# Convolution taps cut to the image, and half of fc1's second half as fifteen quarter-block products with banks that go on as sums

## The chip, the cores and the metric

The kernel runs on one core of one Trainium2 chip. The metric is the device time of one execution in microseconds; before the change its median over three runs is 3315.44 us (3314.96 to 3315.86). All data are float32.

## The reference, cut to what matters

Two layers over 8 images of 384 channels and 32 x 32 pixels (1024 tokens).

```python
# layer 0, per image: attention, then an MLP
xn   = layernorm(x, g1, beta1)
x1   = x + proj(attention(xn))                 # 8 heads of 48
xn2  = layernorm(x1, g2, beta2)
h    = gelu(einsum('bnc,oc->bno', xn2, w_fc1) + b_fc1)     # fc1: 384 -> 1536
x    = x1 + einsum('bnh,oh->bno', h, w_fc2) + b_fc2        # fc2: 1536 -> 384

# layer 1, per image: ConvNeXt block with global response norm
y = conv(x, dw_w, 7x7, padding 3, one filter per channel) + dw_b
y = layernorm over channels(y)
y = gelu(y @ w1 + b1)                          # 384 -> 1536
y = gamma * (y * nx) + beta + y                # nx: norms of the columns over their mean
x = x + (y @ w2 + b2)                          # 1536 -> 384
```

## The kernel before

Tokens lie along the free dimension, channels on the 128 partitions: an image is three channel tiles of 128 x 1024, and `NH` is 512, half of the tokens. The hidden layer is `HT` = 12 tiles of 128 rows. Instructions are issued in program order on each engine. Work of other engines is woven between TensorE's products by a clock in the program (`flow`), which counts the expected TensorE time: `flow.pe(us)` moves it on, and a generator yields the time until its next step. `U` = 0.857 us is one 128 x 128 by 128 x 512 matmul.

The convolution adds one tap at a time on VectorE from a copy of the image with a border of zeros (`pad`). Of the 49 taps, the last seven (`HELPED`) of each channel tile are done by ScalarE (multiply) and GpSimd (a DMA that adds); `taken` keeps VectorE from the channel tile that they are at.

```python
def convolution(acc, us, first=(), y0=0, y1=H, ready=tuple(range(CT)), taken=None):
    done = [0] * CT
    ct, n = None, 0
    taps = KS * KS - (HELPED if taken is not None else 0)
    while min(done) < taps:
        left = [c for c in ready if done[c] < taps and not (taken and taken.get(c, 0) > flow.now)]
        ...
        i = done[ct]
        dy, dx = divmod(i, KS)
        window = pad[:, ct, dy + y0 : dy + y1, dx : dx + W]
        dst = image(acc[:, ct, :])[:, y0:y1, :]
        tap = col("dww", ct * KS * KS + i)
        ...
            nc.vector.scalar_tensor_tensor(dst, window, tap, dst, ALU.mult, ALU.add)
        ...
        yield next((early for m, early in first if n <= m), us)
```

The MLP makes the hidden tiles for the first half of the tokens, then for the second; each half tile is three matmuls into one bank of `ps_o` (four banks), and a gelu on ScalarE. `difference` makes two operands for fc2 ahead of it.

```python
def gelu_half(hid, m, h, xn, weights, wname, name):
    w = weights.at(wname, m // CM)[:, m % CM * CT : (m % CM + 1) * CT, :]
    ps = linear_half(lambda k: w[:, k, :], lambda k: xn[:, k, :], CT, h, f"{name}_{h}_{m}")
    other_table(hid[:, m, half(h)], ps, AF.Gelu, bias=bfc1[:, m : m + 1])

def difference(dst, more, less):
    nc.scalar.mul(dst, less, -1.0)
    nc.gpsimd.dma_start(out=dst, in_=more, accum_op=ALU.add)

def mlp(b, xt, xn, weights, tag, ln, rest, before_fc2=None, behind_ln=None):
    ...
    for m in range(HT):
        gelu_half(hid, m, 0, xn, weights, wa, f"fc1_{b}")
        if m == 3 and rest:
            rest()                  # the projection of the second half, then its norm, ln
            ...
            behind_ln(ln)           # the norm behind the convolution waits for ln
    flow.finish(ln)
    for m in range(HT):
        gelu_half(hid, m, 1, xn, weights, wa, f"fc1_{b}")
        if m % CM == CM - 1:
            weights.used(wa, m // CM)
        if m in (3, 5):
            two_tiles = hid[:, m - 3 : m - 1, :]
            difference(e[(m - 3) // 2], two_tiles[:, :, half(0)], two_tiles[:, :, half(1)])
    ...                             # fc2, by thirds: 15 products of four matmuls for 18
```

The fc2 and w2 products already use sums of weight blocks (15 products for 18); image 0 makes these forms once (`forms`) and stores them. Weights come through a ring of nine buffers (`weights`). The last image (7) has an MLP of its own by halves, and a convolution in two parts of rows (0 to 13, 13 to 32) whose pace is 0.66 and 0.86 us a tap.

Of the kernel before, what the change touches and what calls it, by code (L numbers as in the profile page):

```python
# [46 lines left out]
F32 = mybir.dt.float32  # L47
AF = mybir.ActivationFunctionType
ALU = mybir.AluOpType
# [15 lines left out]
CM = 2  # L65
NC = HT // CM
U = 0.857
HELPED = 7
SCALE = HD ** -0.5
EPS0, EPS1, GRN_EPS = 1e-5, 1e-6, 1e-6  # L70
# [81 lines left out]
def block_kernel(  # L152
# [25 lines left out]
    flow = Flow()  # L178
    quiet = []
    s_fc2 = dram.tile([P, len(FORMS), 4 * P], F32, tag="s_fc2", bufs=1, name="s_fc2")  # L180
    s_w2 = dram.tile([P, len(FORMS), 4 * P], F32, tag="s_w2", bufs=1, name="s_w2")
    s_qk = dram.tile([P, CT, 4 * P], F32, tag="s_qk", bufs=1, name="s_qk")
    s_w1 = dram.tile([P, HT // 2, 4, P], F32, tag="s_w1", bufs=1, name="s_w1")

    def half(h):
        return slice(h * NH, (h + 1) * NH)
# [103 lines left out]
    def chunk(w, c):  # L290
        return w[:, c * 6 * P : (c + 1) * 6 * P]
# [3 lines left out]

    def plan_fc1(tag):
        return [((f"fc1_{tag}", c), chunk(wfc1, c)) for c in range(NC)]

    def plan_fc2(tag):
        return [((f"fc2_{tag}", a), chunk(wfc2, c)) for c, a in enumerate(RAW)]  # L300
# [491 lines left out]
    def add_first(xt, r, n, bank):  # L792
        dst = xt[:, r, half(n)]
        nc.vector.scalar_tensor_tensor(dst, bank, col("bfc2", r), dst, ALU.add, ALU.add)  # L794

    def mlp(b, xt, xn, weights, tag, ln, rest, before_fc2=None, behind_ln=None):

        hid = one.tile([P, HT * N], F32, tag="big", name=f"hid_{b}").rearrange("p (m n) -> p m n", m=HT)
        e = [three.tile([P, 2, NH], F32, tag="p", name=f"fc2_e_{b}_{i}") for i in range(2)]
        wa = f"fc1_{tag}"  # L800
        flow.finish(ln)
        for m in range(HT):
            gelu_half(hid, m, 0, xn, weights, wa, f"fc1_{b}")
            if m == 3 and rest:
                rest()
                slow = 1.2 if b == 1 else 1.0
                ln = flow.spawn(layernorm(xt, xn, 1, eps0, "g2", f"ln2_{b}", True, slow=slow))
                behind_ln(ln)
        flow.finish(ln)
        for m in range(HT):  # L810
            gelu_half(hid, m, 1, xn, weights, wa, f"fc1_{b}")
            if m % CM == CM - 1:
                weights.used(wa, m // CM)
            if m in (3, 5):
                two_tiles = hid[:, m - 3 : m - 1, :]
                difference(e[(m - 3) // 2], two_tiles[:, :, half(0)], two_tiles[:, :, half(1)])
        if before_fc2:
            before_fc2()
        bias = lambda r: col("bfc2", r)
        by_thirds(xt, hid, e, True, weights, f"fc2_{tag}", bias, lambda r, n: pad_half(xt, r, n), f"fc2_{b}")  # L820
# [132 lines left out]
    def keep(b, xt):  # L953
# [2 lines left out]
        nc.sync.dma_start(out=kept.rearrange("(c p) n -> p c n", p=P), in_=xt)  # L956
        return kept

    def convolution(acc, us, first=(), y0=0, y1=H, ready=tuple(range(CT)), taken=None):

        done = [0] * CT
        ct, n = None, 0
        taps = KS * KS - (HELPED if taken is not None else 0)
        while min(done) < taps:
            left = [c for c in ready if done[c] < taps and not (taken and taken.get(c, 0) > flow.now)]
            if not left:
                yield 1.0
                continue  # L970
            ct = min([c for c in left if c != ct] or left, key=lambda c: done[c])
            i = done[ct]
            dy, dx = divmod(i, KS)
            window = pad[:, ct, dy + y0 : dy + y1, dx : dx + W]
            dst = image(acc[:, ct, :])[:, y0:y1, :]
            tap = col("dww", ct * KS * KS + i)
            if i == 0:
                nc.vector.tensor_scalar(dst, window, tap, col("dwb", ct), ALU.mult, ALU.add)  # L978
            else:
                nc.vector.scalar_tensor_tensor(dst, window, tap, dst, ALU.mult, ALU.add)  # L980
            done[ct] += 1
            n += 1
            yield next((early for m, early in first if n <= m), us)

    def help_convolution(acc, us, taken):

        yield 8.0
        for ct in reversed(range(CT)):
            taken[ct] = float("inf")
            for i in range(KS * KS - HELPED, KS * KS):  # L990
                dy, dx = divmod(i, KS)
                for h in range(2):
                    if quiet:
                        while quiet:
                            yield 1.0
                        yield 3.0
                    t = three.tile([P, NH], F32, tag="res", bufs=4, name=f"tap_{ct}_{i}_{h}")
                    y0 = dy + h * H // 2
                    window = pad[:, ct, y0 : y0 + H // 2, dx : dx + W]
                    tap = col("dww", ct * KS * KS + i)  # L1000
                    nc.scalar.mul(t.rearrange("p (h w) -> p h w", w=W), window, tap)  # L1001
                    nc.gpsimd.dma_start(out=acc[:, ct, half(h)], in_=t, accum_op=ALU.add)  # L1002
                    yield us
            taken[ct] = flow.now + 8.0
        yield 8.0
        taken.clear()
# [254 lines left out]
    def prepare(weights, aside):  # L1261
# [17 lines left out]
        def load_blocks(w, name, *which):  # L1279
            t = one.tile([P, CT, N], F32, tag="acc", name=name).rearrange("p c n -> p (c n)")  # L1280
            parts = []
            for j, (m, k) in enumerate(which):
                parts.append(t[:, j * 4 * P : (j + 1) * 4 * P])
                nc.gpsimd.dma_start(out=parts[j], in_=block_of(w, m, k))
            return parts

        def spare(name):
            return three.tile([P, NH], F32, tag="res", bufs=4, name=name)
# [5 lines left out]
            nc.vector.tensor_tensor(dst, x, y, ALU.add)  # L1294

        def forms(name, w, store):
            def keep_form(i, t):
                nc.gpsimd.dma_start(out=store[:, i, :], in_=t)

            a11, a12, a31, a33, a13, a23 = load_blocks(w, f"{name}_a", (1, 1), (1, 2), (3, 1), (3, 3), (1, 3), (2, 3))  # L1300
            x, y, z = (spare(f"{name}_{k}") for k in "xyz")
            yield 16.0
            add(a23, a23, a33)
            add(a11, a11, a12)
            keep_form(6, a11)
            sub(a31, a31, a11)
            keep_form(0, a31)
            yield 2.0
            add(x, a11, a13)
            sub(x, x, a23)  # L1310
            keep_form(8, x)
            nc.vector.scalar_tensor_tensor(y, a11, -1.0, a33, ALU.mult, ALU.subtract)
            keep_form(5, y)
            yield 2.0
            sub(z, a23, a12)
            keep_form(11, z)
            sub(a13, a13, a12)
            sub(a13, a13, a33)
            keep_form(13, a13)
            yield 2.0  # L1320
            nc.vector.tensor_scalar(a12, a12, -1.0, None, ALU.mult)
            keep_form(12, a12)
            nc.vector.tensor_scalar(a23, a23, -1.0, None, ALU.mult)
            keep_form(14, a23)
            a21, a22, a31, a32, a33, a12 = load_blocks(w, f"{name}_b", (2, 1), (2, 2), (3, 1), (3, 2), (3, 3), (1, 2))
            x, y = spare(f"{name}_v"), spare(f"{name}_w")
            nc.gpsimd.dma_start(out=x, in_=block_of(w, 2, 3))
            yield 25.0
            add(x, x, a33)
            sub(y, a22, x)  # L1330
            keep_form(7, y)
            add(a12, a12, a21)
            add(a12, a12, a31)
            keep_form(9, a12)
            yield 2.0
            add(a22, a21, a22)
            sub(a33, a33, a22)
            keep_form(2, a33)
            add(a22, a22, a31)
            keep_form(4, a22)  # L1340
            add(a32, a32, a22)
            keep_form(1, a32)
# [59 lines left out]
        yield 4.0  # L1402
        for j, key in enumerate(order):
            nc.gpsimd.dma_start(out=s_w1[:, :, int(key[1]) - 1, :], in_=t[:, j])
        yield from shift_through_w2()
        yield from forms("w2", w2, s_w2)

# [12 lines left out]
    def main():  # L1420
# [17 lines left out]
        plan = plan_fc1(0) + plan_fc2_fast(0) + plan_qk(1)  # L1438
        for b in range(1, B):
            if b < B - 1:  # L1440
                plan += plan_fc1(b) + plan_fc2_fast(b)
            else:
                for h in range(2):
                    plan += plan_fc1(f"{b}_{h}") + plan_fc2(f"{b}_{h}")
            plan += plan_w1(b - 1, b < B - 1)
            if b == B - 1:
                plan += plan_w1(f"{b}_0", False)
            plan += plan_w2(b - 1, b < B - 1)
            if b < B - 1:
                plan += plan_qk(b + 1)  # L1450
# [74 lines left out]
        for b in range(B):  # L1525
# [22 lines left out]
            flow.finish(state["norm3"])  # L1548
            if b < B - 1:
                y, gx = grn_up(b - 1, acc, weights, b - 1)  # L1550
                start_conv(b, 1.65 if b == B - 2 else 1.7, (26, 2.2), (27, 9.0), (35, 4.4))
                scale = flow.spawn(grn_scale(b - 1, gx, weights, b - 1, y))
                next_values(b + 1)
                flow.finish(scale)
# [166 lines left out]
```

## Time and profile before

| | |
|---|---|
| median of 3 runs | 3315.44 us |
| profiled span | 3315.9 us |
| TensorE busy | 3279.8 us (99%) |
| VectorE busy | 2511.5 us (76%) |
| ScalarE busy | 1604.1 us (48%) |
| GpSimd busy | 484.2 us (15%) |
| convolution taps of 128 x 1024 on VectorE | 861, 1276 ns each |
| fc1 matmul records | 1152 of 128 x 512 |

How to read it: times are microseconds unless marked ns. PE is TensorE's matmuls, PEld its weight loads, DVE is VectorE, ACT ScalarE, POOL GpSimd, SP the engine that issues most loads. An f32 matmul stands in the trace as two records. A group's row has: line of the kernel, engine, operation, out<-in by tile names, shapes, count, then busy us and mean ns of one, then the idle time before it and what ended it. PEclk is the share of full clock that TensorE was granted. A wait's row has the waiting engine and line, what it waited for, total us, times and the longest.

### The profile page before, as it was taken

Reading aid. Unit: us, or ns where it says so; the run is one execution under the profiler, and the core shown is the slowest. Engines: PE = TensorE matmul, PEld = TensorE weight load, DVE = VectorE, ACT = ScalarE, POOL = GpSimd, SP = SyncE. Lnnn points to the kernel's source line nnn. Section 1 sums busy time; section 2 is a strip of 40 time slices with the busy share of each in tenths; the row PEclk is TensorE's granted clock in tenths of the full one; section 3 lists DMA queues with packets and bytes.
Section 4 is the critical chain, followed back from the end, with each engine's and each line's share of the span. In section 5 each row is a group of like instructions: output and inputs, shape, how many; then the busy total and the mean of one; then the engine's idle time right before and its main releaser. Section 6 shows DMA issues by size and latency. Waiting matters only on the chain. (4 is left out here: it accounts for less than half of the span.)

```text
span 3315.9 us, 38765 instructions
## 1 busy us (share of the span) xinstructions
PE 3279.8 (99%) x14296; PEld 1415.0 (43%) x14296; DVE 2511.5 (76%) x3186; ACT 1604.1 (48%) x2194; POOL 484.2 (15%) x569
## 2 busy tenths in 40 slices
PE   8999999999999999999999999999999999999998
PEld 4344434443344433444344443444434443444455
DVE  4444897888867978679786798768886888879940
ACT  2542663447534375353652737526473355623541
POOL 2121210112110121101211022111220112100000
PEclk9999999999999999999999999999999999999999
DMA  5336732657244563537436373273742647333231
GB/s 197 112 106 147 150 68 71 156 115 150 56 104 135 137 127 58 131 106 172 84 58 148 103 187 70 58 179 84 175 78 50 180 106 160 63 74 89 69 95 43
DMA packets 199109, 368.73 MB, mean 111 GB/s; under 512 B 40768, under 2 KB 46784, under 8 KB 198528
## 3 DMA queue, kind: packets, MB, share of 16 engines
q0 software_dynamic: 80896, 158.63, 26.3%
q1 hardware_dynamic: 117728, 206.83, 20.7%
q8 instruction: 115, 1.88, 0.2%
q10 hardware_dynamic: 288, 0.71, 0.1%
q14 instruction: 82, 0.67, 0.1%
HBM read 187.03 MB, written 34.60 MB: 67 GB/s over the span
## 5 line engine op out<-in xcount | busy, mean ns | idle before, releaser
L980 DVE SCALAR_TENSOR_TENSOR acc<-pad,vec,acc 128x1024 f32<-128x1024 f32 x861 | 1069.3, 1276 | 20.1 <-DMA acc<-tap 15.5
L673 ACT ACTIVATE p<-s 128x1024 f32<-128x1024 f32 x512 | 523.8, 1023 | 278.5 <-PE s L664 270.1
L664 PE MATMUL s<-qk 48*64 48x512 f32 x4096 | 544.7, 593 | 0.8 <-ACT p L673 0.6
L684 PE MATMUL o<-p,v 64*64 64x512 f32 x4096 | 541.2, 591 | 0.0
L351 PE MATMUL fc<-xn,fc 128*128 128x512 f32 x1152 | 504.0, 596 | 4.8 <-DVE acc L423 4.8
L1002 POOL DMA_DIRECT2D acc<-tap x294 | 253.7, 884 | 1212.2 <-ACT tap L1001 747.9
L351 PEld LDWEIGHTS fc<-xn,fc 128*128 128x128 f32 x1152 | 219.2, 191 | 285.6 <-issue 275.7
L358 PE MATMUL fc_p<-hid,fc 128*128 128x512 f32 x728 | 318.6, 594 | 0.2 <-DMA hid<-hid 0.2
L370 ACT ACTIVATE hid<-fc,bfc_f 128x512 f32<-128x512 f32 x192 | 131.5, 686 | 348.0 <-PE fc L351 347.6
L684 PEld LDWEIGHTS o<-p,v 64*64 64x64 f32 x4096 | 165.5, 133 | 278.3 <-issue 266.7
L664 PEld LDWEIGHTS s<-qk 48*64 48x64 f32 x4096 | 161.2, 133 | 278.6 <-issue 220.5
L358 PE MATMUL o_p<-y,w 128*128 128x512 f32 x624 | 272.3, 593 | 0.0
L1051 DVE TENSOR_TENSOR y<-h,y 128x512 f32<-128x512 f32 x288 | 197.0, 690 | 90.8 <-PE h L358 76.2
L1001 ACT ACTIVATE tap<-pad,vec 128x512 f32<-128x512 f32 x294 | 210.9, 727 | 25.4 <-DMA acc<-tap 25.2
L358 PEld LDWEIGHTS fc_p<-hid,fc 128*128 128x128 f32 x728 | 137.2, 190 | 179.0 <-issue 166.5
L358 PE MATMUL h<-acc,w_A 128*128 128x512 f32 x432 | 207.3, 595 | 0.0
L980 DVE SCALAR_TENSOR_TENSOR wqkv<-pad,vec,wqkv 128x416 f32<-128x416 f32 (+1 forms) x288 | 193.5, 744 | 0.5
L358 PEld LDWEIGHTS o_p<-y,w 128*128 128x128 f32 x624 | 117.5, 190 | 150.6 <-issue 129.1
L790 ACT COPY pad<-x 128x512 f32<-128x512 f32 x48 | 30.2, 635 | 251.0 <-DVE x L856 187.0
L625 DVE TENSOR_TENSOR attn<-o,attn 128x512 f32<-128x512 f32 x64 | 44.1, 689 | 138.6 <-ACT attn L623 138.6
L549 DVE TENSOR_TENSOR qk<-qk,qk 128x512 f32<-128x512 f32 x168 | 111.5, 686 | 29.0 <-PE qk L358 20.0
L592 PE MATMUL v<-wqkv,xn 128*128 128x384 f32 x384 | 128.2, 491 | 0.0
(311 smaller groups left out, 3751.4 us busy)
## 6 DMA issues: line engine op xcount, KB each, us to landing
acc<-tap POOLq DMA_DIRECT2D x294, 256.0 KB, 3.5
w_A<-in_w SPq DMA_DIRECT2D x72, 384.0 KB
fc<-s_fc SPq DMA_DIRECT2D x91, 256.0 KB
hid<-hid POOLq DMA_DIRECT2D x42, 512.0 KB, 7.1
fc<-in_wfc SPq DMA_DIRECT2D x54, 384.0 KB
w<-s_w SPq DMA_DIRECT2D x78, 256.0 KB
y<-y POOLq DMA_DIRECT2D x36, 512.0 KB, 6.8
kept<-x SPq DMA_DIRECT2D x8, 1536.0 KB
```

The source lines that it names most:

```text
L351: nc.tensor.matmul(out=ps, lhsT=lhsT(k), rhs=rhs(k)[:, half(h)], start=(k == 0), stop=(k == nk - 1))
L358: nc.tensor.matmul(out=bank, lhsT=lhsT, rhs=rhs, start=k == 0, stop=k == len(pairs) - 1)
L370: nc.scalar.activation(dst, src, function, **kw)
L549: nc.vector.tensor_tensor(dst, bank, part, ALU.add)
L592: nc.tensor.matmul(out=ps[:, :C], lhsT=xn[:, k, t * P : (t + 1) * P], rhs=wv_sb[:, k, :], start=(k == 0), stop=(k == CT - 1),)
L664: nc.tensor.matmul(out=s[64 * i : 64 * i + 64, j, :], lhsT=kT[64 * j : 64 * j + HD, m, k0 : k0 + 64], rhs=qT[64 * j : 64 * j + HD, m, half ...
L673: nc.scalar.activation(p, s, AF.Exp)
L684: nc.tensor.matmul(out=outs[i][64 * j : 64 * j + 64, :], lhsT=v[keys, t, at : at + 64], rhs=p[keys, j, :], start=(t == 0), stop=(t == KT - 1),
L980: nc.vector.scalar_tensor_tensor(dst, window, tap, dst, ALU.mult, ALU.add)
L1001: nc.scalar.mul(t.rearrange("p (h w) -> p h w", w=W), window, tap)
L1002: nc.gpsimd.dma_start(out=acc[:, ct, half(h)], in_=t, accum_op=ALU.add)
L1051: nc.vector.tensor_tensor(dst, bank, part, ALU.add)
```

## The change

**Taps.** A tap is added only where the shifted image lies inside: a window of up to 32 x 32 that is up to three rows and three columns smaller. The centre tap, which covers everything, comes first; the seven taps that ScalarE and GpSimd help with are now the middle column's, which still use the whole rows. The paces of the convolutions of images 1 to 6 are set tighter.

**fc1.** For images 1 to 6, in the second half of the tokens, the first six of the twelve hidden tiles are made in two groups of three tiles. A group is a product of 3 x 3 weight blocks with 3 x 2 blocks of 256 tokens, done in 15 matmuls of 256 columns rather than 18 (nine of 512). It needs ten sums of token blocks (`quarter_sums`, VectorE), fifteen forms of the weights, made in image 0 and kept in memory (`s_fc1`), and adds that put the outputs together. To save adds, a bank that has been read goes on as a sum: the next product is accumulated on top of it. The aim is less work for TensorE, with the VectorE time that the shorter taps leave.

```diff
+FAST = 2
+    s_fc1 = dram.tile([P, 4, len(FORMS), P], F32, tag="s_fc1", bufs=1, name="s_fc1")
...
+    def fc1_group(hid, group, xn, sums, weights, wname, name, late):
...
+        def product(i, ps, more=False):
+            w = weights.at(wname, group, i // 6)[:, i % 6, :]
+            nc.tensor.matmul(out=ps, lhsT=w, rhs=right[i], start=not more, stop=True, skip_group_check=more)
+            flow.pe(U / 2)
+            return ps
...
+        y = product(6, bank("y"))
+        nc.scalar.copy(c11, y)
+        t = product(2, bank("t"))
+        nc.scalar.mul(c21, t, -1.0)
+        x = product(0, bank("x", True))
+        nc.scalar.copy(n16, x)
+        z = product(10, bank("z"))
+        product(5, y, True)
+        lately()
+        product(1, t, True)
+        op(n16, y, n16)
+        x = product(3, bank("u", True))
+        op(c32, x, n16)
+        v_ = product(12, bank("v"))
+        op(c32, c32, z, ALU.subtract)
+        x = product(4, bank("w", True))
+        lately()
+        op(n17, x, n16)
+        op(c31, t, n17)
+        product(13, y, True)
+        nc.scalar.copy(c12, y)
+        op(c12, c12, z, ALU.subtract)
+        op(c12, c12, v_)
+        lately()
+        product(11, v_, True)
+        x = product(14, bank("q", True))
+        op(c11, v_, c11)
+        product(9, v_, True)
+        op(c21, x, c21)
+        product(7, z, True)
+        product(8, x, True)
+        op(n17, v_, n17, ALU.subtract)
+        op(c22, z, n17)
+        op(c21, c21, n17)
+        op(c11, x, c11)
...
+        late += [gelu(2), gelu(1), gelu(0)]          # in place, ScalarE, done later
...
     def mlp(...):
+        fast = FAST if isinstance(b, int) and b > 0 else 0
...
+                making = flow.spawn(after(ln, quarter_sums(xn, sums), 1)) if fast else None
...
+            for g in range(fast):
+                for _ in range(2 if g == 0 else HT - 3 * fast - 5):     # 2, then 1 plain tile
+                    m = next(plain)
+                    gelu_half(hid, m, 1, xn, weights, wa, f"fc1_{b}")
...
+                fc1_group(hid, g, xn, sums, weights, f"fc1f_{tag}", f"fc1_{b}", late)
+                if g == 1:
+                    late.append(lambda: difference_of(0))
...
+            for m in plain:                                             # the last 3 tiles
...
+            if fast < 3:
+                difference_of(1)
...
     def convolution(...):
+        shares = [size(*divmod(i, KS), y0, y1) for i in TAPS[:taps]]
+        shares = [taps * s / sum(shares) for s in shares]
...
-            dy, dx = divmod(i, KS)
-            window = pad[:, ct, dy + y0 : dy + y1, dx : dx + W]
-            dst = image(acc[:, ct, :])[:, y0:y1, :]
-            tap = col("dww", ct * KS * KS + i)
+            dy, dx = divmod(TAPS[i], KS)
+            rows, cols = inside(dy, dx, y0, y1)
+            window = inner(ct)[:, rows.start + dy - PAD : rows.stop + dy - PAD, cols.start + dx - PAD : cols.stop + dx - PAD]
+            dst = image(acc[:, ct, :])[:, rows, cols]
+            tap = col("dww", ct * KS * KS + TAPS[i])
...
-            yield next((early for m, early in first if n <= m), us)
+            yield share * next((early for m, early in first if n <= m), us)
...
     def help_convolution(acc, us, taken):
-            for i in range(KS * KS - HELPED, KS * KS):
+            for i in TAPS[KS * KS - HELPED :]:
...
+        yield from forms("fc1", wfc1, s_fc1)                            # image 0
...
-                plan += plan_fc1(b) + plan_fc2_fast(b)
+                plan += plan_fc1(b) + plan_fc1_fast(b) + plan_fc2_fast(b)
...
-                start_conv(b, 1.65 if b == B - 2 else 1.7, (26, 2.2), (27, 9.0), (35, 4.4))
+                start_conv(b, 1.55 if b == B - 2 else 1.58, (26, 2.1), (27, 9.0), (35, 4.4))
```

## The prediction, before the run

> **What bounds the kernel now.** I read the page's first part, the windows of 50 us, then TensorE's waits, and only then single groups.
>
> ```profile
> PE 3279.8 (99%) x14296; PEld 1415.0 (43%) x14296; DVE 2511.5 (76%) x3186; ACT 1604.1 (48%) x2194; POOL 484.2 (15%) x569
> ```
> ```profile
> core 0: us, PE busy (x) PEld busy (x) DVE busy (x) ACT busy (x) POOL busy (x), PEclk, DMA share, GB/s
> ...
> 1700.00:1750.00 50.00, 50.00 (x118) 22.10 (x117) 40.74 (x46) 18.85 (x27) 3.34 (x4) 1.00 0.16 34
> ...
> 2950.00:3000.00 50.00, 45.19 (x109) 18.74 (x109) 47.19 (x76) 12.69 (x19) 3.25 (x4) 0.93 0.31 74
> ...
> 3150.00:3200.00 50.00, 44.23 (x106) 21.74 (x105) 38.66 (x58) 7.63 (x16) 0.00 (x0) 0.90 0.26 74
> ```
> TensorE is full in nearly every window of images 1 to 6; it idles at the start, at the end and in the last image. A busy PE row may hide small gaps, so I looked at start-to-start times as well: the passes follow each other without a hole. Hence the middle gets shorter only by fewer TensorE columns, and any new TensorE wait there is added to the time in full. The waits view has only two that matter outside the first 20 us:
>
> ```profile
> engine line waited for: us in total, times, longest us
> ...
> PE fc L351 <- DVE acc L423: 4.8, 1, 4.8
> ...
> PE h_last L1150 <- DVE wqkv L451: 1.6, 1, 1.6
> ```
>
> **The durations I use.** PE timeline in the last stage, ten records of 288 columns and the next ten:
>
> ```profile
> 3251.00 2.59 PE L1106 MATMUL o<-y_x,w_A 128*128 128x288 f32 x10
> 3253.43 2.59 PE L1106 MATMUL o<-y_acc,w_A 128*128 128x288 f32 x10
> ```
> (3253.43-3251.00)/10 = 0.243 us a record. An f32 matmul leaves two records. For 512 columns the weight loads below give 0.43 (0.429 on average). The Trainium skill, "TensorE: Matmul & The Clock Gate", section "Back-to-back issue gap", gives N/2.4 + 2.5 ns; the trace agrees if N is twice the columns of a record (576/2.4+2.5 = 242.5 ns; 1024/2.4+2.5 = 429 ns). So my estimate for 256 columns is 0.216 us a record, 0.432 a matmul; the weight load of 0.19 just fits under it.
>
> ```profile
> 941.22 0.19 PEld L351 LDWEIGHTS fc<-xn,fc 128*128 128x128 f32 x1 [0.24 <-issue]
> 941.65 0.19 PEld L351 LDWEIGHTS fc<-xn,fc 128*128 128x128 f32 x1 [0.24 <-issue]
> ...
> 941.85 0.69 ACT L370 ACTIVATE hid<-fc,bfc_f 128x512 f32<-128x512 f32 x1 [1.89 <-PE fc L351]
> ```
> The product's last record ends where the next one starts, at 941.65; the reader starts at 941.85. TensorE to reader: 0.20 us. Groups by shape:
>
> ```profile
> L980 DVE SCALAR_TENSOR_TENSOR acc<-pad,vec,acc 128x1024 f32<-128x1024 f32 x861 | 1069.3, 1276 | 20.1 <-DMA acc<-tap 15.5
> L1051 DVE TENSOR_TENSOR y<-h,y 128x512 f32<-128x512 f32 x288 | 197.0, 690 | 90.8 <-PE h L358 76.2 <-ACT y L1053 9.4
> L980 DVE SCALAR_TENSOR_TENSOR wqkv<-pad,vec,wqkv 128x608 f32<-128x608 f32 x144 | 110.5, 844 | 0.0
> L980 DVE SCALAR_TENSOR_TENSOR wqkv<-pad,vec,wqkv 128x416 f32<-128x416 f32 x144 | 83.0, 644 | 0.5
> ```
> From 416 and 608: (844-644)/192 = 1.042 ns an element, 210 ns fixed (checks: 1024 gives 1277). A 256-wide VectorE add: the skill's "VectorE: DVE Perf Modes", section "The TRN2 errata — SBUF-src ops pay a fixed extra latency per instruction", has (N+151)/0.96 for fp32 tensor_tensor; the trace agrees at 512 (690.6 against 690), so 256 takes about 424 ns. ScalarE copies take 581 ns at 512 and 477 at 384 (the attention and value copies), so about 0.37 us at 256. VectorE to TensorE, the last norm:
>
> ```profile
> 3184.19 0.46 DVE L416 TENSOR_TENSOR ln_a<-ln_a,wqkv 128x288 f32<-128x288 f32 x1
> 3184.70 0.30 PEld L380 LDWEIGHTS ln_sum<-ln_a,ones 128*128 128x128 f32 x2 [2.53 <-DVE ln_a L416]
> ```
> about 0.06 us, and the first record after the wait is some 0.1 us long of step.
>
> **The change, part by part.**
>
> *Fewer columns.* Six images (1 to 6) times two groups. A group was 9 matmuls of 512 (18 records x 0.429 = 7.72 us) and becomes 15 of 256 (30 x 0.216 = 6.48). 12 x 1.24 = **-14.9 us**. This is all that the middle can win.
>
> *New waits.* Follow the bank `v`. Product 12 opens it; `c12` adds it; only then may product 11 go on in it. The skill, "PSUM — Partial Sum Buffer", section "PSUM bank collisions raise a hardware error", says that a bank's readers and TensorE's writes have to be ordered by semaphores, by bank. So TensorE, which runs in program order, stands between product 13 and product 11 for this chain: product 13 to ScalarE 0.20, copy to c12 0.37, to VectorE 0.03, c12 minus z and c12 plus v 2 x 0.43, to TensorE 0.06, restart 0.10: **1.62 us** with nothing for TensorE between. Then product 9 needs c11 (which reads v after product 11): 0.20+0.42+0.06+0.10 = 0.78, less product 14 in between, 0.43: **0.35 us**. The other going-on banks have two or more products between (y: three; t: three; z and q enough). 12 x 1.97 = **+23.6 us**. A group thus costs 6.48+1.97 = 8.45 us against 7.72.
>
> *Taps between those adds.* VectorE now finishes the convolution here:
>
> ```profile
> 930.91 15.81 DVE L980 SCALAR_TENSOR_TENSOR acc<-pad,vec,acc 128x1024 f32<-128x1024 f32 x12
> 946.76 0.69 DVE L413 TENSOR_TENSOR ln_a<-acc 128x512 f32<-128x512 f32 x1
> ```
> The second half of fc1 starts near 936.5 (31 us before fc2's first product at 968.5). These twelve taps come late because ScalarE and GpSimd hold one channel tile until their own last tap (923), so the faster pace (1.58 for 1.70) brings their end forward by a few us only. In the new order some ten remain, one every 1.55 us, across group 0, which runs 5 to 13 us into the half. VectorE keeps program order: about one tap of 1.16 us lands between the adds on which product 11 waits. I take 1.3 us for group 0 of each image: **+7.8 us**. Group 1 should meet the norm's first adds only at its start: nothing.
>
> *The clock.* After a long wait TensorE ran at half clock:
>
> ```profile
> 2979.00:2985.30 6.30, 6.11 (x7) 2.52 (x8) 5.88 (x11) 2.90 (x6) 0.00 (x0) 0.50 0.00 0
> ```
> The skill's TensorE page, section "What's actually happening", explains it by windows of 3413 ns in which TensorE was idle; the 4.8 us wait before it and the 6.3 us at half clock agree with such windows. A group's 2 to 3 us of holes may fill most of one. If three of twelve do, at 1.7 us: **+5 us**.
>
> *Convolution.* A tap off the middle column now has 906 elements on average (212/7 rows x 30 columns, less one tap) for 1024: 41 x 3 x 118 x 1.042 ns = 15 us less VectorE an image. The ten sums and 26 group adds put 36 x 0.42 = 15 us back. Neither is on TensorE's path in the middle. In the last image it is: the 4.8 us wait is for acc L423, behind 12 taps of conv 6 and some 26 taps of 416. They lose 12 x 0.12 + 26 x 0.05 = 2.7 us, and one or two taps come earlier (1.8): nearly the whole wait, and with it perhaps the half clock after it (3.4): **-6.5 us**. The holes of 3183 to 3191 stay: the last convolution's pace (0.66, 0.86) is not changed, its shares average to one, and that norm starts only after the last down-projection block's add.
>
> *Rest.* The second difference for fc2 is now made after the last gelu; ScalarE 0.7 + 1.05, then GpSimd 1.2 and some 5 us to land, against 8.6 us until TensorE wants it: **+2** in all six. The extra forms of fc1 in image 0: 15 stores in pieces of 512 bytes and some twenty adds more, while attention has room, **+1**.
>
> Sum: 3315.4 - 14.9 + 23.6 + 7.8 + 5 - 6.5 + 3 = 3333. I shade it to **3330 us**, since the half-clock term is a guess that can only be zero or positive and the tap term may be smaller.
>
> **Rivals.** (a) The waits are hidden and only the columns count: 3315.4 - 14.9 - 6.5 = 3294 to 3302. For it: every other product in this kernel reads out without TensorE noticing. Against it: those products are four matmuls long (3.4 us), these are 0.43 us, and nothing stands between 13 and 11. (b) VectorE becomes the bound of fc1's second half: ten taps, norm and 26 adds in 30 us. Before, VectorE was busy there for 12.65 of 31 us; with 11 us of adds it has some 24. Full only locally; if the norm's six subtractions or ScalarE's six squares fall into group 1, 3 us an image more: 3348. (c) The new wait halves the clock in most groups: 12 x 1.7 = 20 for my 5: 3345. (d) The weights come late: 15 more blocks of 64 KB a group, into a stage with little traffic (DMA share 0.15 in the windows from 897.8 to 936.5); I give it nothing.
>
> **Range and chances.** Low is (a) half right, with the last image's wait gone: 3304. High is (b) or (c): 3347. Two per cent is 66 us; neither the saved columns (15) nor all of the rivals reach that. Faster by 2%: 0.01; within: 0.96; slower: 0.03.
>
> **What would show it.** Records of fc1 with 256 columns 0.216 us apart inside a group; in TensorE's waits a new first row, fc1's bank on VectorE's add, 12 times or more at 1.6 us and over; PE busy a little under 99%; VectorE's total nearly unchanged; taps of about 1.15 us; the granted clock below 1.00 in some windows of fc1; the wait on acc L423 near 2979 small. I am wrong if the group's records follow each other without a hole, or if a group lasts under 7.7 us.

## The result: 3375.66 us, 1.8% more than before, and above the predicted range

The changed kernel takes 3375.66 us (median of 4 runs, 3374.22 to 3378.07). The kernel before took 3315.64 us beside it, so that the ratio is 1.0182 (95% interval 1.0164 to 1.0200). Predicted were 3330 us, with 3304 to 3347 as the range.

The first part of the page of the kernel after, then the first two rows of its waits (us in total, times, longest us) and its taps:

```profile
PE 3285.9 (97%) x14440; PEld 1468.8 (44%) x14440; DVE 2487.2 (74%) x3422; ACT 1618.3 (48%) x2242; POOL 505.0 (15%) x597
```
```profile
PE fc_p L367 <- DMA fc_e<-hid: 28.9, 6, 5.5
PE fc_v L837 <- DVE hid L842: 23.5, 12, 2.9
```
```profile
L1136 DVE SCALAR_TENSOR_TENSOR acc<-pad,vec,acc 128x899 f32<-128x899 f32 (+8 forms) x861 | 962.7, 1155 | 10.6 <-DMA acc<-tap 7.5
```
TensorE went from 99% to 97%; VectorE does no more than before. The second wait was predicted: bank `v`, on the add that reads it, in all 12 groups. The first and largest was not: fc2 waits for one of its two differences, once in each of six images. The wait on `acc` in the last image is gone.

TensorE's timeline in image 5 holds both groups. First the holes before product 11 (group 0 above, group 1 below; time and duration in us, the idle time in brackets):

```profile
2202.04 1.22 PE L837 MATMUL fc_v<-hid,fc1f 128*128 128x256 f32 x2 [2.32 <-DVE hid L842]
...
2214.39 0.70 PE L837 MATMUL fc_v<-hid,fc1f 128*128 128x256 f32 x2 [1.37 <-DVE hid L842]
```
VectorE, in the hole of group 0:

```profile
2199.26 1.15 DVE L1136 SCALAR_TENSOR_TENSOR acc<-pad,vec,acc 128x899 f32<-128x899 f32 x1
...
2201.12 0.41 DVE L842 TENSOR_TENSOR hid<-hid,fc_z 128x256 f32<-128x256 f32 x1
2201.56 0.42 DVE L842 TENSOR_TENSOR hid<-hid,fc_v 128x256 f32<-128x256 f32 x1
```
Product 13 starts at 2199.13. A tap, and two adds for other outputs, run ahead of the two adds that product 11 needs in VectorE's queue; the last add ends at 2201.98 and TensorE starts at 2202.04. Both hole and tap are as the prediction had them.

Now fc2 of the same image. One product there is eight records: the first four read the first difference, the other four the second, and that one is not there in time. Below it the issues of that operand (POOL) and of the next image's load (SP, two transfers of 768 KB) are shown:

```profile
2232.82 1.88 PE L367 MATMUL fc_p<-fc_e,fc 128*128 128x512 f32 x4
2239.50 3.68 PE L367 MATMUL fc_p<-fc_e,fc 128*128 128x512 f32 x4 [4.81 <-DMA fc_e<-hid]
```
```profile
2226.56 1.90 SPq L198 DMA_DIRECT2D xn<-in_x  x2
...
2228.08 1.18 POOL L795 DMA_DIRECT2D fc_e<-hid  x1 [2.59 <-ACT fc_e L794]
```
The same two in image 2 of the kernel before, where the difference landed 8.5 us before the load began (5.4 us after its own issue):

```profile
954.08 1.19 POOL L786 DMA_DIRECT2D fc_e<-hid  x1 [3.96 <-ACT fc_e L785]
...
968.00 0.92 SPq L196 DMA_DIRECT2D xn<-in_x  x2
```
From issue to landing the differences of all images, 512 KB each, took, in microseconds (before, then after):

```profile
DMA to landing us min/median/max: 5.2/5.2/6.5
```
```profile
DMA to landing us min/median/max: 5.2/6.7/12.1
```
Windows of 3.4 us around the hole of group 0 and the hole of fc2 (after the stretch come length, busy time of PE, PEld, DVE, ACT and POOL, the granted clock, the DMA share and GB/s):

```profile
2198.60:2202.00 3.40, 1.12 (x6) 0.64 (x4) 3.28 (x7) 0.37 (x1) 0.00 (x0) 1.00 0.28 77
2202.00:2205.40 3.40, 3.36 (x8) 2.53 (x9) 2.10 (x4) 0.00 (x0) 0.00 (x0) 0.50 0.07 11
2236.10:2239.50 3.40, 0.00 (x0) 0.00 (x0) 0.02 (x1) 0.00 (x0) 0.00 (x0) 1.00 1.11 263
2239.50:2242.90 3.40, 3.40 (x4) 1.51 (x5) 1.21 (x1) 0.00 (x0) 0.00 (x0) 0.51 0.29 80
```
The DMA engines are full while TensorE waits in fc2 (share 1.11; a packet counts with its whole time where it starts, so that a share can pass 1), and each hole is followed by 3.4 us at half clock. The Trainium skill, "TensorE: Matmul & The Clock Gate", section "HAM oscillation — how this bites in real kernels", warns of idle gaps over some 3.4 us and counts half of a throttled stretch as lost. The half agrees: four records of fc2 take 3.68 us there and 1.88 at full clock. The gap does not: in the first pair an idle time of 2.32 us was enough, with TensorE busy for 1.12 of the 3.40 us. The measurement decides.

Nor does the length of the hole settle it. Group 0 has the same hole of 2.3 us in images 2, 3, 4 and 6, and no half clock behind it. All nine stretches at half clock in images 1 to 6 start at whole multiples of 3.413 us from one another: from 560.18 to 573.84 it is 4 of them, to 2202.00 it is 481. In image 4 a boundary of this grid, 1792.40, cuts the hole in two:

```profile
1788.99:1792.40 3.41, 1.60 (x8) 1.07 (x6) 2.99 (x6) 0.37 (x1) 0.00 (x0) 1.00 0.28 75
1792.40:1795.81 3.41, 2.59 (x10) 1.66 (x11) 2.54 (x5) 0.00 (x0) 0.00 (x0) 1.00 0.20 44
```
In images 1 to 6 of this trace, every step of the grid at full clock in which TensorE was idle for 2.1 us or more was followed by half clock (nine), and none in which it was idle for 1.8 us or less. So the same hole costs half clock or not by where it falls on the grid.

Where the difference of the two profiled runs (3372.7 - 3315.9 = 56.8 us) lies, from the first products of each stage:

| stage | after - before, us | predicted |
|---|---|---|
| image 0 | +11.3 | +1 |
| fc1, images 1 to 6 | +7.24 +3.04 +3.04 +3.03 +3.85 +3.04 = +23.2 | -14.9 + 23.6 + 7.8 + 5 = +21.5 |
| fc2, images 1 to 6 | +7.90 +6.36 +6.65 +6.51 +6.66 +6.39 = +40.5 | +2 |
| last image, from its fc1 | -13.5 | -6.5 |
| the rest, by difference | -4.7 | 0 |

### The profile page after: what moved, and what is told of

The parts are those of the page before. It is cut to its first block, busy times and chain, and to the rows that moved or that the text cites. A ratio compares the mean times of both kernels' runs of the same rounds, so it can differ in the third digit from the quotient of the medians.

```text
span 3372.7 us, 39491 instructions
## 1 busy us (share of the span) xinstructions
PE 3285.9 (97%) x14440; PEld 1468.8 (44%) x14440; DVE 2487.2 (74%) x3422; ACT 1618.3 (48%) x2242; POOL 505.0 (15%) x597
## 4 chain that ended last, share of the span: by engine, by line
PE 87%; issue 3%; DMA 2%; DVE 1%; ACT 0%; POOL 0%; POOLq 0%; ACTq 0%; DVEq 0%
PE fc L360 12%; PE s L673 12%; PE o L693 12%; PE h L367 10%; PE o_p L367 9%; PE fc_p L367 9%; PE qk L367 6%; PE o L1262 4%; PE v L601 3%; PE proj L615 3%; DMA fc_e<-hid 2%; PE h_last L1306 2%; PE h L347 2%; DVE hid L842 1%; PE ln_var L403 1%
## 5 line engine op out<-in xcount | busy, mean ns | idle before, releaser
L1136 DVE SCALAR_TENSOR_TENSOR acc<-pad,vec,acc 128x899 f32<-128x899 f32 (+8 forms) x861 | 962.7, 1155 | 10.6 <-DMA acc<-tap 7.5
L673 PE MATMUL s<-qk 48*64 48x512 f32 x4096 | 552.1, 592 | 0.2 <-ACT qk L514 0.2
L693 PE MATMUL o<-p,v 64*64 64x512 f32 x4096 | 548.8, 591 | 0.0
L360 PE MATMUL fc<-xn,fc 128*128 128x512 f32 x936 | 412.1, 594 | 0.0
L693 PEld LDWEIGHTS o<-p,v 64*64 64x64 f32 x4096 | 177.0, 133 | 267.5 <-issue 253.2
L673 PEld LDWEIGHTS s<-qk 48*64 48x64 f32 x4096 | 171.8, 133 | 268.5 <-issue 210.6
L360 PEld LDWEIGHTS fc<-xn,fc 128*128 128x128 f32 x936 | 176.4, 190 | 222.5 <-issue 204.6
L379 ACT ACTIVATE hid<-fc,bfc_f 128x512 f32<-128x512 f32 x156 | 106.7, 687 | 343.8 <-PE fc L360 343.7
L1136 DVE SCALAR_TENSOR_TENSOR wqkv<-pad,vec,wqkv 128x377 f32<-128x377 f32 (+24 forms) x288 | 177.3, 690 | 0.6
```

Of the source, the lines that this page charges most:

```text
L360: nc.tensor.matmul(out=ps, lhsT=lhsT(k), rhs=rhs(k)[:, half(h)], start=(k == 0), stop=(k == nk - 1))
L673: nc.tensor.matmul(out=s[64 * i : 64 * i + 64, j, :], lhsT=kT[64 * j : 64 * j + HD, m, k0 : k0 + 64], rhs=qT[64 * j : 64 * j + HD, m, half ...
L693: nc.tensor.matmul(out=outs[i][64 * j : 64 * j + 64, :], lhsT=v[keys, t, at : at + 64], rhs=p[keys, j, :], start=(t == 0), stop=(t == KT - 1),
```

## The experiments

Theory A: fc2's wait comes from contention; the late difference meets the load of the next image. Rival B: it comes from the difference being late in itself, or fc2 has another limit. Beside it stand the sizes of the other parts: taps, image 0's forms, the groups. E1 to E4 peel the change off part by part. In E1, E2, E9, E11 and E12 `FAST = 0` makes all hidden tiles in the old way. E1 to E4 ran on one chip, E5 to E8 on a second, E9 to E11 on a third and E12 on a fourth, where the kernel before took 3317.40, 3316.82, 3316.34 and 3316.58 us; a difference between runs of two chips is uncertain by about 1 us.

**E1: the taps alone.**

```diff
-FAST = 2
+FAST = 0
-        yield from forms("fc1", wfc1, s_fc1)
```


> Taps inside the image and the new paces alone: no fc1 groups, no forms of fc1 in image 0. Theory (the middle is bound by TensorE, so shorter taps gain only in the last image, where the wait of 4.8 us and the half clock after it go): about 3306 us, 3302 to 3311; each middle image as long as before, fc1 to fc2 of the last image about 32.4 us for 40.3. Rival (the taps or their paces lose something in the middle and are part of the 60 us): over 3316 us.

Measured: 3305.74 us (3304.31 to 3306.92), beside 3317.4 us before on that chip; ratio 0.9965 (0.9952 to 0.9977). The taps alone win 11.7 us. The way from fc1 to fc2 in the last image fell from 40.2 to 32.4 us, which is about the wait of 4.8 and what the 6.8 us at half clock behind it had cost (3.4); the remaining 3 to 4 us are spread over the other stages, some half a microsecond an image.

**E2: taps, and image 0's forms of fc1, which nobody uses.**

```diff
-FAST = 2
+FAST = 0
```


> As the run with the taps alone, but image 0 makes and stores the forms of fc1, which nothing reads. Theory (the forms cost image 0 the 11.3 us that it got longer): 11 us over the taps alone, about 3317 us, with a wait of TensorE on the norm's fold by DMA near 166 us. Rival (image 0 got longer by something else): within 3 us of the taps alone.

Measured: 3313.06 us (3307.86 to 3316.46), ratio 0.9989 (0.9982 to 0.9995): 7.3 us over E1, less than the 11 that the theory had and more than the rival's 3. Its row of the waits that grew from E1's 0.8 us:

```profile
PE ln_sum L403 <- DMA ln_a<-ln_a: 6.2, 2, 5.0
```
TensorE waits for the fold of image 0's second norm, and the trace has half clock from 170.3 and 306.8 on. Image 1's value products start at 339.9 us for 330.9. In the change they start at 342.2: there TensorE also waits 1.7 us at 323.75, with 6.8 us at half clock behind it, which E2 lacks. What holds it up there was not tried.

**E3: the next image's load 16 us later.**

```diff
-                xn = state["xn"] = load_x(b + 1, "xn")
+                xn = state["xn"] = load_x_later(b + 1, 16.0) if 0 < b < B - 1 else load_x(b + 1, "xn")
```
`load_x_later` issues the same two transfers from a generator that first yields 16 us.

> The changed kernel, with the next image's load (1.5 MB) issued 16 us into fc2 rather than at its start; the differences for fc2 stay late. Theory A (that load holds up the adding DMA of the second difference): TensorE's wait on it falls from 28.9 us in 6 to under 6 us, fc2 of a middle image from 59.3 to about 53 us, the time to 3336 to 3345. Theory B (the difference is simply started too late, its DMA is as fast as it can be): over 3365 us, landing still near 11 us.

Measured: 3353.34 us (3350.35 to 3355.36), ratio 1.0107 (1.0090 to 1.0123), between the two theories. The wait on `fc_e<-hid` fell from 28.9 to 2.4 us, and the difference landed within 7.5 us at most: what had delayed it was the load. But the load now meets fc2's adding transfers:

```profile
PE fc_p L379 <- DMA hid<-hid: 8.3, 6, 1.5
```
Their longest time to landing went from 12.1 to 15.9 us. Half clock is gone from fc2; it came in seven of the twelve groups instead of three, behind the same holes. A was right on the cause, and too hopeful on the cure: moving the load moves the collision.

**E4: the differences earlier.** The groups' gelus are done in reverse order, each difference as soon as its two tiles are there.

```diff
                 if g == 1:
-                    late.append(lambda: difference_of(0))
+                    late = [lambda: difference_of(0), late[2], lambda: difference_of(1), late[1], late[0]]
...
-            if fast < 3:
-                difference_of(1)
```


> The changed kernel, with the two differences issued some 5 to 8 us earlier (right after the gelus that they need), the next image's load where it was. Theories A and B both expect the wait on the difference to go: 3334 to 3342 us, fc2 of a middle image about 53 us. If it stays over 3360, the wait is for something else than the time at which the difference is started. Group times stay: about 10.7 us for group 0 and 8.5 for group 1.

Measured: 3335.05 us (3333.10 to 3337.14), ratio 1.0052 (1.0035 to 1.0068), 40.6 us under the change. fc2 takes the time of before; in image 5 the eight records that read the two differences follow without a hole:

```profile
2206.12 3.60 PE L367 MATMUL fc_p<-fc_e,fc 128*128 128x512 f32 x8
```
The second difference is issued at 2195.77 there, 4.1 us ahead of the load at 2199.86, and lands 5.0 us after its issue. The order of the two, and not the work, made the 40.6 us.

**E5: E4, and other products between 12's adds and 11.** Order 12, 13, 4, 14, 7, 11, 8, 9 for 12, 4, 13, 11, 14, 9, 7, 8; the adds follow their products, those on `c12` first.

```diff
         v_ = product(12, bank("v"))
         op(c32, c32, z, ALU.subtract)
-        x = product(4, bank("w", True))
-        lately()
-        op(n17, x, n16)
-        op(c31, t, n17)
         product(13, y, True)
         nc.scalar.copy(c12, y)
+        w = product(4, bank("w", True))
+        q = product(14, bank("q", True))
         op(c12, c12, z, ALU.subtract)
         op(c12, c12, v_)
         lately()
+        product(7, z, True)
         product(11, v_, True)
...
```


> Early differences as before, and the products of a group in another order: 13, 4, 14, 7, 11, 8, 9, so that TensorE has three products of 0.43 us between product 13 and the one that goes on in bank v, and one between 11 and 9. Theory (a group loses its 2 us to the order, not to columns of 256): group 1 from 8.5 to 7.0 to 7.3 us, group 0 from 10.7 to 8.0 to 9.0, waits on the bank v from 23.5 us to under 8; 23 us less than with early differences alone: 3309 to 3317 us. Rival (VectorE has too much to do there, whatever the order): groups within 0.7 us of what they were, over 3328 us.

Measured: 3319.02 us (3312.39 to 3323.17), ratio 1.0005 (0.9996 to 1.0013), 16.0 us under E4, where 23 were expected. Group 1 fell from 8.47 to 7.24 us, group 0 from between 9.9 and 10.8 to 8.65 (images 2 to 6). None of the groups runs at half clock any more; in E4 five do, so the gain is not the holes' alone. The wait for `v` is replaced by smaller ones at the two other banks that go on:

```profile
PE fc_z L837 <- DVE hid L842: 6.0, 7, 1.7
...
PE fc_q L837 <- DVE hid L842: 3.4, 5, 0.7
```
The 12 groups last 97.1 us (5 x 7.24 + 5 x 8.65, and 8.4 and 9.26 in image 1), 8.09 on average, against 7.72 for three plain tiles. Even so ordered, the fifteen products lose.

**E10: E4, and product 11 in a bank of its own.** The order stays; product 9 goes on in that bank, and two more adds on VectorE join what was one sum.

```diff
+        v2 = product(11, bank("v2", True))
+        x = product(14, bank("q", True))
+        op(c11, v2, c11)
         op(c12, c12, z, ALU.subtract)
         op(c12, c12, v_)
         lately()
-        product(11, v_, True)
-        x = product(14, bank("q", True))
         op(c11, v_, c11)
-        product(9, v_, True)
+        product(9, v2, True)
...
         op(n17, v_, n17, ALU.subtract)
+        op(n17, v2, n17)
```


> Early differences (3335.1 us) and product 11 in a bank of its own, where product 9 then goes on; two more adds of 0.42 us on VectorE in a group, the order of the products as in the change. Theory (TensorE waits for the reader of the bank that goes on): group 1 goes from 8.47 to 7.0 to 7.3 us, the wait fc_v on VectorE is gone, 3316 to 3322 us. Rival (VectorE's amount of work in the group sets it): group 1 stays at 8 us or more, 3333 us or more.

Measured: 3323.57 us (3321.83 to 3327.68), ratio 1.0021 (1.0013 to 1.0029): 11.5 us under E4, a little short of what was expected. Group 1 is 7.41 us although VectorE has more to do. The wait for `v` is gone but for 2.3 us in image 1. The hole went to the next bank that goes on:

```profile
PE fc_q L837 <- DVE hid L842: 9.0, 12, 1.4
...
PE fc_q L837 <- DVE fc_n L842: 4.2, 6, 1.0
```
So in group 1 TensorE waits for the reader of a bank that goes on, and it is not the amount of VectorE's work that holds it. The groups last 102.6 us here (5 x 7.41 + 5 x 9.37, and 8.9 and 9.82 in image 1), 8.55 on average; in E4 they last 115.8, 9.65 on average.

**E6: the whole change with the old taps and paces.**

```diff
-            dy, dx = divmod(TAPS[i], KS)
-            rows, cols = inside(dy, dx, y0, y1)
...
+            dy, dx = divmod(i, KS)
+            window = pad[:, ct, dy + y0 : dy + y1, dx : dx + W]
+            dst = image(acc[:, ct, :])[:, y0:y1, :]
...
-                start_conv(b, 1.55 if b == B - 2 else 1.58, (26, 2.1), (27, 9.0), (35, 4.4))
+                start_conv(b, 1.65 if b == B - 2 else 1.7, (26, 2.2), (27, 9.0), (35, 4.4))
```


> The changed kernel with the old convolution and its old paces: fc1's part alone. Theory (the shorter taps gain some 10 us in the last image and lie less in the way of the group's adds): 3385 to 3402 us, with the hole of fc1 in the last image back, and group 0 longer than 10.7 us. Rival (the new taps are part of the loss): at or under 3376 us.

Measured: 3424.93 us (3420.24 to 3434.57), ratio 1.0323 (1.0307 to 1.0338), 49 us over the change: far more than expected. Its wait for bank `v`:

```profile
PE fc_v L837 <- DVE hid L842: 38.5, 13, 4.1
```
The expectation looked for the loss in group 0. That one lasts 9.6 to 10.9 us in images 2 to 6, much as in the change; it is group 1 that went from 8.47 to 12.9 us. With the longer taps and the old paces the convolution ends later, and its norm falls into group 1: in image 5 four steps of the norm (L422 and L425, from 2250.09 to 2252.82) stand in VectorE's queue ahead of the two adds that product 11 needs. The profile is of the slowest of the four runs, 60.1 us longer than the change's (3432.8 for 3372.7). The wait for `v` is 15 us of that, the wait of 4.8 us in the last image is back, and TensorE stood at half clock for some 131 us, against 63 in the change, at a cost of half the difference, 34 us; some 6 us are spread over other stages. The shorter taps with their paces are worth 11.7 us to the old fc1 and 49 to the new one.

**E7: E5, with shorter pauses in image 0's forms of fc1 and w2.** Its aim was the 7 us of E2.

```diff
-            yield 16.0
+            yield 16.0 if w is wfc2 else 12.0
...
                 keep_form(10, a33)
+                yield 8.0
...
-            yield 25.0
+            yield 25.0 if w is wfc2 else 17.0
```


> Early differences, the new order, and image 0's forms of fc1 and w2 with shorter pauses, the second load of fc1's blocks put behind the norm's fold. Theory (image 0 loses its 7 to 11 us to that fold's DMA behind the loads, and to loads in fc2): 4 to 8 us under the run with the new order alone: 3302 to 3311 us, faster than the kernel before, but not clearly than the taps alone (3306). Rival (the extra forms cost image 0 about 7 us wherever they lie): within 2 us of the new order alone.

Measured: 3313.07 us (3309.59 to 3316.46), ratio 0.9990 (0.9984 to 0.9997), 6 us under E5 and 2 above what was expected. Image 1's value products start at 335.2 us for 344.5 in E5 (330.9 before), and image 0 has no half clock behind 170 any more. So some 6 us of what the forms cost was their timing. Which of the forms' loads, stores and adds it is that holds the fold back was not separated. E7 is the change with each part mended, and still some 7 to 8 us behind the taps alone.

**E8: E7 with three groups (`FAST = 3`).** With nine tiles in groups, the plain tiles before the first group are written over four of the ten token sums, so the products take other data; the instructions are those of three groups.

```diff
-FAST = 2
+FAST = 3
```


> As the run with all three, with three groups instead of two (nine of the twelve hidden tiles). Theory: a group of 7.0 to 7.3 us replaces 7.72 us of plain products, so a third group gains 6 x 0.5 = 3 us: 2 to 5 us under the run with all three. Rival (with one plain tile less between groups the adds of one group meet the next one's): 5 us or more over it.

Measured: 3329.84 us (3329.15 to 3332.88), ratio 1.0044 (1.0028 to 1.0059), 16.8 us over E7. The time is as the rival had it, the reason is another one. In images 2 to 5 the three groups take 8.65, 9.8 and 7.24 us: the third gains its 0.5 us on three plain tiles, and the second has a new hole of 2.3 us before product 13, which waits for the add that reads bank `y`. VectorE just before it, then TensorE, in image 5:

```profile
2176.95 0.69 DVE L425 TENSOR_TENSOR attn<-attn,acc 128x512 f32<-128x512 f32 x1
2177.56 0.42 DVE L842 TENSOR_TENSOR fc_n<-fc_y,fc_n 128x256 f32<-128x256 f32 x1
```
```profile
2178.03 0.70 PE L837 MATMUL fc_y<-xn,fc1f 128*128 128x256 f32 x2 [2.31 <-DVE fc_n L842]
```
The adds of the first group had ended at 2173.86. Behind them VectorE did the last tap of the convolution and four steps of its norm, without a pause from 2173.78 to 2177.64; the first row shown is the last of these steps. With no plain tile between the first two groups the second one comes 2.6 us earlier and meets them.

**E9: E1 with a tighter pace in the last image.** There VectorE waits for the program's clock, and the norm of the lower rows waits for VectorE.

```diff
-                conv = convolution(last, 0.86 if h else 0.66, (), *rows, ready[h])
+                conv = convolution(last, 0.79 if h else 0.63, (), *rows, ready[h])
```


> Taps alone (3305.7 us), with the last image's convolution set to 0.63 and 0.79 us a tap for 0.66 and 0.86. Theory: with the shorter taps VectorE waits for the pace in the last image (busy some 120 of the 138 us before 3178), and the norm of its lower rows begins only behind the last down-projection block; a tighter pace closes the holes of 1.7, 2.4 and 1.6 us at 3171 to 3179 and the half clock behind them (3.4 us): about 3297 us (3294 to 3301). Rival (VectorE cannot follow, or the norm shows at another place): 3304 us or more.

Measured: 3298.28 us (3297.18 to 3299.71), beside 3316.34 before on that chip; ratio 0.9945 (0.9931 to 0.9959), as expected: 7.5 us under E1, or 6.4 when each is taken against the kernel before on its chip. Of E1's holes of 1.70, 2.44 and 1.62 us between 3172 and 3179 only one of 1.3 us is left, and the half clock behind them (6.8 us long in E1) is gone.

**E11: E9 with a still tighter pace.**

```diff
-                conv = convolution(last, 0.79 if h else 0.63, (), *rows, ready[h])
+                conv = convolution(last, 0.74 if h else 0.58, (), *rows, ready[h])
```


> The same with 0.58 and 0.74 us a tap. Theory (only the pace holds the norm back): as with 0.63 and 0.79, within 2 us. Rival (VectorE falls behind, and the adds that empty TensorE's banks stand behind taps in its queue): 4 us or more above that run, with waits of TensorE on VectorE's y adds in the last image.

Measured: 3306.38 us (3304.36 to 3307.19), ratio 0.9969 (0.9957 to 0.9981), 8.1 us over E9. VectorE falls behind, as the rival had it, though the wait is for the norm's sums more than for the `y` adds it named. TensorE, and VectorE in the 14 us before:

```profile
3046.28 1.48 PE L389 MATMUL ln_sum<-ln_a,ones 128*128 128x416 f32 x2 [2.51 <-DVE ln_a L425]
```
```profile
3032.66 9.59 DVE L1136 SCALAR_TENSOR_TENSOR wqkv<-pad,vec,wqkv 128x403 f32<-128x403 f32 x18
...
3045.63 0.59 DVE L425 TENSOR_TENSOR ln_a<-ln_a,wqkv 128x416 f32<-128x416 f32 x1
```
Eighteen taps in a row, and a few instructions more, stand in VectorE's queue ahead of the two adds that TensorE needs.

**E12: the first part as in E9, the second as in E11.**

```diff
-                conv = convolution(last, 0.79 if h else 0.63, (), *rows, ready[h])
+                conv = convolution(last, 0.74 if h else 0.63, (), *rows, ready[h])
```


> Taps alone with 0.63 us a tap in the first part of the last image's convolution (as in the 3298.3 us run) and 0.74 in the second (as in the 3306.4 us run). Theory: the loss of 8 us lay in the first part, where VectorE is full and the adds that TensorE waits for stand behind taps; the second part has room: 3295 to 3299 us, and the last wait of TensorE on wqkv L460 (1.3 us at 3175) is gone. Rival (the second part's pace is what costs): 3303 us or more.

Measured: 3298.53 us (3296.64 to 3300.20), ratio 0.9947 (0.9934 to 0.9961). The loss of E11 lay in the first part. The second part's pace is worth nothing beyond E9: the last hole on `wqkv` (1.3 us) is gone, but TensorE now waits 1.6 us for ScalarE at 3109.81, which it does not in E9. E9 and E12 are the fastest of all versions: the shorter taps with a fitting pace in the last image, and fc1 left alone.

The change taken apart: each kernel differs from the one above it by one part. The rows sum to the whole by construction, and another order would share it out differently, as E6 shows for the taps. The first four ran on one chip; the change ran on another, where the kernel before took 3315.64 us, so the last row may be off by 2 us:

| from | to | what it adds | us |
|---|---|---|---|
| before, 3317.4 | E1, 3305.74 | taps | -11.7 |
| E1 | E2, 3313.06 | image 0's forms | +7.3 |
| E2 | E4, 3335.05 | twelve groups of fifteen products | +22.0 |
| E4 | the change, 3375.66 | differences late, into the next image's load | +40.6 |

## Why the prediction was wrong

**The step that failed** is in "Rest": "The second difference for fc2 is now made after the last gelu; ScalarE 0.7 + 1.05, then GpSimd 1.2 and some 5 us to land, against 8.6 us until TensorE wants it: +2 in all six." Its other terms hold. In image 5 the last gelu starts at 2226.15, GpSimd issues at 2228.08, and TensorE wants the operand at 2239.50 - 4.81 = 2234.69, 8.5 us after the gelu's start. The landing does not hold: issue to landing was some 11.4 us (2228.08 to 2239.5) instead of 1.2 + 5, because 1.5 MB for the next image had been issued 1.5 us ahead. The Trainium skill, "DMA: Bandwidth & Descriptors", section "Issuing engines are not separate DMA queues", says that transfers from whatever engine run on the same 16 DMA engines and interleave; the trace agrees, with a DMA share of 1.11 in the wait, and E3 and E4 show it from both sides. The prediction took 5 us from the transfers of the kernel before (5.2 us, at DMA shares of 0.74 to 0.82), which were issued 14 us ahead of that load, and did not ask what else is issued when fc1 ends. It mattered twice: 28.9 us of waiting, and then 23.9 us at half clock in fc2 of images 1 to 6, at a cost of 12. Their sum, 40.9, is the 40.5 us of the table.

**Image 0's forms**, "while attention has room, +1": TensorE has no room in image 0 where the fold of the second norm comes late. E2 has 7.3 us in place of the 1, the change 11.3, and E7 shows that other pauses give back some 6 of what E5 spends there.

**fc1 was right in its mechanism, and its sum in part by luck.** In images 2 to 6 group 1 lasts 8.47 us (8.45 worked out) and group 0, where no half clock comes, 9.92 (9.75 worked out); the tap between the adds is there, records are 0.216 us apart, and a tap takes 1155 ns. Half clock came in three of twelve groups, from 560.2, 573.8 and 2202.0 us on, the very number of the guess; but behind the same holes it came in five groups of E4 and in seven of E3. In image 5 it made the stage only 0.8 us longer than in image 4, for the 1.7 taken. Image 1, which the sum took to be like the others, makes up for that with its +7.24. The stage gave +23.2 us for +21.5, and E4 less E2 gives +22.0.

**The rivals.** (a), hidden waits, is refuted by the 23.5 us of the new row. (b) named what came in E6 and E8, where the norm's steps fell into a group, which then lasted 12.9 and 9.8 us; in the change they meet only the start of group 1 (2207.86 to 2210.61 in image 5), at no cost, as the prediction had it. (c), half clock in most groups, was not so in the change, though it was in E3; half clock in fc2 stood in none of the rivals. (d), late weights, shows in no wait.

**The last image** was right in its mechanism and too small: -6.5 for -13.5. The wait of 4.8 us and the half clock behind it are wholly gone (7.9 us); the other 5.6 us lie in the tail, where the prediction left everything as it was, and 3.1 of them are half clock that was 6.2 us shorter there. The prediction's "only two" waits after the first 20 us left out two more of the last norm: together with the 1.6 us on `wqkv`, TensorE waits 1.70, 2.45 and 1.62 us between 3183 and 3191. That "the last convolution's pace is not changed", and so these holes stay, held in E1; it should have been read as an offer, and E9 takes 6 to 7.5 us from it.

**The range** failed because its upper end came from rivals within fc1 alone. In fc1, where each term was worked out from a chain of durations, the sum came out within 2 us; the two terms in "Rest" that got a small round number were off by 6 to 10 and by 39.

## What to carry to other kernels

A transfer that is moved later has to be priced beside what else starts at the new time: with its duration apart from that, and its duration behind the largest load issued within a few microseconds before it. A bank that goes on as a sum saves an add, and makes TensorE wait for the whole chain of its reader unless products of at least that length stand between. Whatever else stands in the reader's queue at that moment is added to the chain: here a tap of 1.15 us in group 0, and four steps of a norm, 2.7 us, in E6 and E8. Try the reordering and a bank of its own before counting the columns saved. When an engine other than the bottleneck gets faster, look at what paces it: the programmed pace, and not the engine's speed, held 6 to 7.5 us here.

## What was not expected of the hardware

- A hole of 2.3 us brought 3.4 us at half clock in image 5 and none in images 2, 3, 4 and 6; what differed is how it fell on a grid of 3.413 us. In images 1 to 6 the trace has nine stretches at half clock, 34.1 us in all: three in groups (10.2 us) and six behind fc2's wait (23.9 us), none elsewhere.
- A SBUF transfer that adds 512 KB takes 5.2 us in the median of the kernel before, and 10.6 to 12.1 where a load of 1.5 MB was issued 1.5 to 2.1 us ahead of it.
- In E6 a wait that was 15 us longer in total came with some 68 us more at half clock, which cost 34 us, more than twice the waiting itself.
